# A four-layer convolution network on one core: weight preparation reordered, interval right products on two row tiles, Newton roots for the norms, image parts in eight transfers

## The chip, the cores and the metric

The kernel runs on one core of a Trainium2 chip. The time is the device time of one execution in microseconds (us). Three executions of the kernel before took 2478.43, 2479.14 and 2481.91 us; the median, 2479.14 us, is the number that the changed kernel is compared with.

A core has a matrix engine (PE), a vector engine (DVE), a scalar engine (ACT) and a general engine (POOL). Each works through its own list of instructions in order; where an instruction waits for a result of another engine, everything behind it on its own list waits too. SP, a fifth list, does no arithmetic: it issues nearly all DMA transfers of this kernel, also in order.

## The reference

The input x has 4 batches of 32x32 positions with 16 channels. Four layers each add to x a function of its group norm `_gn(x)` (8 groups of 2 channels; each group is divided by the square root of its variance plus 1e-5). Layers 0, 1 and 3 are convolutions in which every output position has its own 3x3x16x16 kernel G:

```python
first = jnp.einsum('ijyx,byxc->bijc', Msq, inputs)
...
diff = jax.nn.relu(inputs[:, None, None, :, :, :] - shifted)
second = L * jnp.einsum('ijyx,bijyxc->bijc', Wsq, diff)
return first - second
```

Here `shifted` is, for each of the 1024 output positions and each channel, a whole 32x32 image: the input convolved with the kernel of that position. Layer 3 (the last) does the same with another order of the axes of the input. Layer 2 is a dynamic program over intervals. Running maxima and minima over all intervals give a table r; two steps follow of the form `max over k of sigmoid(f[i,k] Wf + r[k,j] Wr + b)`, and then one last sigmoid of a product. The products with Wr are called right products below, those with Wf left products.

## The kernel before, in words

**Phases and steps.** The three convolution layers are done for two pairs of batches g (NG = 2): six phases, in the order (g, layer) = (0,0), (1,0), (0,1), (1,1), (0,2), (1,2). A phase has 8 chunks t of 128 output positions, and a chunk has 32 steps: 16 channels f times 2 images b. So there are 1536 steps. A step fills one PSUM tile of 128 positions x 1024 pixels (a pair of banks; four such tiles exist, tag "ps"). DVE then multiplies min(tile, 0) by the chunk's W and sums, in one instruction with its accumulator read (`second_part`, L680).

**A step on PE.** For accuracy, weights and images are split into an upper part and a remainder in the faster matmul type. `first_part` issues 8 matmuls with the image parts `ib` and `ia`; ACT then scales the PSUM tile in place (L663); `second_part` adds 6 matmuls with `iyz` and `im9`. All have 64 rows of contraction: they come in pairs, one on the upper and one on the lower half of the array's rows (a row tile each). `conv_layer` issues first_part of step k, then second_part of step k-1, so the scaling of one step hides behind the matmuls of its neighbours. The first 16 steps (units 0 and 1, "plain") use unsplit fp32 data and are longer.

**Units and slots.** The weights of 4 channels of one chunk are a unit u; a unit serves 8 steps. The generator `prep_parts` (L220) prepares the units two ahead. It is resumed once per step, so that a unit takes 8 steps, which are called slots 1 to 8 here. Slot 1: DVE cuts off the upper bits (L203). Slot 2: ACT L175. Slot 3: ACT L236, POOL L237 and L238. Slot 4: ACT L240, POOL L241 and four copies (L243, L245). Slot 5: POOL subtracts the identity from the raw weights of unit u+1 (`prep`, L214). Slot 7: SP moves a part to the other half of the partitions (L251, two transfers) and loads the raw weights of unit u+2 (`load_raw`, L110, 768 KB, into the buffer that unit u has just left).

**What runs behind.** All else runs as a second generator, `behind(phase)`, resumed at the end of a step. Its `yield n` waits n steps; `yield IDLE` waits for slot 1, 5, 6, 7 or 8, `yield CALM` for slot 6, 7 or 8. Behind a phase it makes the images of the next one: `group_norm` (L312), a turn of the result and its way through DRAM (L375 to L395), then per image b `split`, `place` and `difference`. Behind phases 3 and 4 it first does the interval layer (`interval_layer`, L484) for g = 0 and 1. The products with M come through `first_terms` (L418) behind phases 0, 2 and 5.

**The parts that the diff touches.** `place` (L290) copies quarters of the split image into `ia` and `ib` with 12 transfers per image. `group_norm` gets the variance sums on DVE (the last instruction is the transpose at L337), takes a square root on ACT (L358, after a one-element square root at L353 that pulls the function table in early), a reciprocal on DVE (L360) and multiplies on POOL (L361). The interval layer uses sigmoids on ACT, with a one-element one at L591 for the same reason. Its `right_side` (L555) makes three fp32 products of 352, 231 and 110 columns, one in each of three successive steps, each in its own PSUM tile and all on the upper row tile (L561), and ACT copies each into the table `rt` (L564). Steps of a chunk run through f, and within it through b; only the very first chunk is sorted so that 4 channels of image 0 come before those of image 1.

The norms whose sums end in slot 5 are those of the first two convolution layers (the waits between their parts are 4 steps). Those of the interval layer (waits of 2) and of the last convolution layer (waits of 1) end in slot 2.

Of the kernel before, what the change touches and what calls it, by code (L numbers as in the profile page):

```python
# [15 lines left out]
P = 128  # L16
# [3 lines left out]
GC = GB * C  # L20
# [24 lines left out]
def net_kernel(ctx: ExitStack, tc: tile.TileContext, x, xq, xi, convs, iv_w, iv_b, out):  # L45
# [174 lines left out]
    def prep_parts():  # L220
# [4 lines left out]
        for u in range(PLAIN, n_chunks * NU):  # L225
# [12 lines left out]
            nc.gpsimd.tensor_tensor(W9, W9.bitcast(F32), src[:, 2], ALU.add)  # L238
            yield ()
# [4 lines left out]
            for lo, hi in QUARTERS:  # L244
                nc.gpsimd.tensor_copy(WL[lo], high[hi])  # L245
            yield ()
            prep(u + 1)
# [7 lines left out]
            load_raw(u + RAWS)  # L255
# [14 lines left out]
    def halves(temp, b):  # L270
        v = temp.rearrange("p (k s b n) -> p k s b n", k=2, s=2, b=GB)
        return v[:, 0, :, b], v[:, 1, :, b]
# [36 lines left out]
    def pair_view(ap):  # L309
        return ap.rearrange("p t (g s) -> p t g s", s=2)  # L310

    def group_norm(g, name, dst, gap):  # L312
# [47 lines left out]
        nc.vector.reciprocal(rstd, rstd)  # L360
# [7 lines left out]
    def before_conv(g, layer):  # L368
# [29 lines left out]
        temp = big.tile([P, 8192], F32R, tag="big", name=f"temp_{g}{layer}")[:, :TEMP]  # L398
# [19 lines left out]
    def first_terms(layer, mt):  # L418
# [3 lines left out]
        for g in range(NG):  # L422
            for pt in range(NT):
                for j in range(4):
# [4 lines left out]
                    )  # L429
        ft = work.tile([P, NG, NT * GC], F32, tag="fs", name=f"ft_{layer}")  # L430
# [15 lines left out]
    def constants():  # L446
# [7 lines left out]
        nc.gpsimd.tensor_scalar_mul(mask2[GC : 2 * GC], mask2[GC : 2 * GC], -1.0)  # L454
# [23 lines left out]
        for k, name in ((1, "r0"), (4, "r1")):  # L478
            t = const.tile([64, NQ * GB, C], F32, name=name)
# [4 lines left out]
    def interval_layer(g):  # L484
# [56 lines left out]
        )  # L541
        yield 5
# [437 lines left out]
```

## Time and profile before

| what | us |
|---|---|
| three runs, median | 2479.14 |
| the profiled execution, its own time | 2478.41 |
| its span, first to last instruction | 2476.7 |
| PE matmul busy | 2458.2 |
| DVE busy | 2087.3 |
| ACT busy | 1878.4 |
| POOL busy | 1579.7 |
| L680, the mean of one of 1536 | 1.224, and 0.083 for the accumulator read |
| L663, the mean of one of 1520 | 1.008 |

"Busy" is the part of the span in which an engine worked. Matmuls are pipelined and their ends are modelled, so a PE that is busy at 99% may still run slower than it could: the starts of successive matmuls tell more. In an undisturbed stretch of the trace (starts from 537.66 to 935.74 us, 254 steps) a step takes 1.567 us. In the timeline a row gives start, duration, engine, line, operation, output <- inputs, and in brackets the idle time before it with what ended that.

### The profile page before, as it was taken

Reading aid. Unit: us, or ns where it says so; the run is one execution under the profiler, and the core shown is the slowest. Engines: PE = TensorE matmul, PEld = TensorE weight load, DVE = VectorE, ACT = ScalarE, POOL = GpSimd, SP = SyncE. Lnnn points to the kernel's source line nnn. Section 1 sums busy time; section 2 is a strip of 40 time slices with the busy share of each in tenths; the row PEclk is TensorE's granted clock in tenths of the full one; section 3 lists DMA queues with packets and bytes.
Section 4 is the critical chain, followed back from the end, with each engine's and each line's share of the span. In section 5 each row is a group of like instructions: output and inputs, shape, how many; then the busy total and the mean of one; then the engine's idle time right before and its main releaser. Section 6 shows DMA issues by size and latency. Waiting matters only on the chain.

```text
span 2476.7 us, 58058 instructions
## 1 busy us (share of the span) xinstructions
PE 2458.2 (99%) x21906; PEld 2090.1 (84%) x21906; DVE 2087.3 (84%) x3617; ACT 1878.4 (76%) x2181; POOL 1579.7 (64%) x1750
## 2 busy tenths in 40 slices
PE   8999999999999999999999999999999999999999
PEld 5999888888888888888888988888998888888887
DVE  9888878888888888778898988899889888788887
ACT  4778767787777778777777777787777787677776
POOL 4766655666565657555567777586878676555552
PEclk9999999999999999999999999999999999999999
DMA  6446754466454467644454545574455467554442
GB/s 198 138 137 182 203 155 135 124 182 164 133 143 135 135 168 198 186 116 134 136 145 127 142 124 140 146 196 125 126 138 144 127 181 195 154 148 137 137 137 54
DMA packets 97673, 366.92 MB, mean 148 GB/s; under 512 B 26480, under 2 KB 31472, under 8 KB 97392
## 3 DMA queue, kind: packets, MB, share of 16 engines
q1 hardware_dynamic: 96832, 362.79, 53.0%
q8 instruction: 172, 2.82, 0.5%
q14 instruction: 109, 0.89, 0.1%
q10 hardware_dynamic: 432, 0.39, 0.1%
q0 software_dynamic: 128, 0.02, 0.0%
HBM read 199.78 MB, written 1.02 MB: 81 GB/s over the span
## 4 chain that ended last, share of the span: by engine, by line
PE 94%; DVE 2%; issue 1%; DMA 1%; ACT 0%; SPq 0%; POOL 0%; ACTq 0%; DVEq 0%; POOLq 0%
PE pc L627 93%; DVE junk L680 1%; PE pf L425 1%; DMA raw<-in_g 1%; ACT pc L663 0%; DMA first<-in_g 0%; SPq L298 0%; DVE raw L846 0%; SPq L300 0%; PE ps_l L548 0%; PE ps_r L561 0%; DMA parts<-parts 0%; DVE tables L508 0%; DVE raw L854 0%; DMA ib<-first 0%
## 5 line engine op out<-in xcount | busy, mean ns | idle before, releaser
L680 DVE SCALAR_TENSOR_TENSOR junk<-pc,WT 128x1024 f32<-128x1024 f32 x1536 | 1879.5, 1224 | 359.1 <-PE pc L627 308.3
L663 ACT ACTIVATE pc<-pc 128x1024 f32<-128x1024 f32 x1520 | 1532.0, 1008 | 561.0 <-PE pc L627 535.8
L627 PE MATMUL pc<-ib,parts 64*128 64x512 f32 x6080 | 958.5, 388 | 4.1 <-DVE junk L680 3.4
L627 PE MATMUL pc<-iyz,parts 64*128 64x512 f32 x6080 | 955.5, 387 | 2.2 <-ACT pc L663 2.0
L627 PE MATMUL pc<-ia,parts 64*128 64x496 f32 x6080 | 933.5, 379 | 0.0
L627 PEld LDWEIGHTS pc<-ia,parts 64*128 64x128 f32 x6080 | 595.5, 184 | 100.8
L627 PEld LDWEIGHTS pc<-ib,parts 64*128 64x128 f32 x6080 | 591.5, 184 | 105.0 <-DVE junk L680 9.9
L627 PEld LDWEIGHTS pc<-iyz,parts 64*128 64x128 f32 x6080 | 592.5, 184 | 88.4 <-ACT pc L663 6.4
L627 PE MATMUL pc<-im,W 64*128 64x496 f32 x3072 | 611.5, 384 | 0.0
L237 POOL TENSOR_TENSOR parts<-raw,upper_w 128x512 fp32r<-128x512 f32 x190 | 248.5, 1308 | 500.2 <-DVE upper_w L203 434.8
L627 PEld LDWEIGHTS pc<-im,W 64*128 64x128 f32 x3072 | 303.0, 184 | 54.5 <-issue 3.2
L243 POOL CAST parts<-parts 32x512 fp32r<-32x512 f32 x380 | 231.1, 608 | 50.1 <-ACT parts L240 31.8
L238 POOL TENSOR_TENSOR W<-W,raw 128x512 fp32r<-128x512 f32 x190 | 247.6, 1303 | 1.8 <-ACT W L175 1.8
L241 POOL TENSOR_TENSOR parts<-parts 128x512 fp32r<-128x512 f32 x190 | 246.8, 1299 | 2.0 <-ACT parts L236 1.9
L245 POOL CAST parts<-upper_w 32x512 fp32r<-32x512 f32 x380 | 231.6, 609 | 22.8
L214 POOL TENSOR_TENSOR raw<-raw,ident 128x512 f32<-128x512 f32 x190 | 199.9, 1052 | 52.2 <-DMA raw<-in_g 28.7
L175 ACT ACTIVATE W<-raw,low_w 128x512 fp32r<-128x512 f32 x190 | 136.2, 717 | 0.1
L680 DVE DVE_READ_ACCUMULATOR junk<-pc,WT 128x1 f32 x1536 | 127.5, 83 | 0.0
L236 ACT ACTIVATE parts<-upper_w 128x512 fp32r<-128x512 f32 x190 | 118.8, 625 | 6.6 <-DVE upper_w L203 6.4
L240 ACT CAST parts<-upper_w 128x512 fp32r<-128x512 f32 x190 | 116.5, 613 | 0.0
L695 POOL TENSOR_SCALAR acc<-acc 128x32 f32<-128x32 f32 x40 | 16.4, 409 | 141.7 <-DVE junk L680 139.7
L203 DVE TENSOR_SCALAR upper_w<-raw 128x512 int32<-128x512 int32 x190 | 86.1, 453 | 1.2 <-POOL raw L214 0.9
(139 smaller groups left out, 479.4 us busy)
## 6 DMA issues: line engine op xcount, KB each, us to landing
raw<-in_g SPq DMA_DIRECT2D x190, 768.0 KB, 7.1
parts<-parts SPq DMA_DIRECT2D x380, 384.0 KB, 4.9
WT<-in_w SPq DMA_DIRECT2D x48, 512.0 KB, 4.6
MT<-in_mt SPq DMA_DIRECT2D x24, 512.0 KB, 7.4
raw<-xs SPq DMA_DIRECT2D x120, 71.8 KB, 2.9
ib<-temp SPq DMA_DIRECT2D x40, 128.0 KB, 2.6
ia<-temp SPq DMA_DIRECT2D x80, 62.0 KB, 3.4
ib<-first SPq DMA_DIRECT2D x8, 128.0 KB, 2.4
```

Source lines behind the costliest of these rows:

```text
L175: nc.scalar.activation(dst, src, AF.Copy, scale=mask[:, 1:2])
L214: eng.tensor_tensor(raws[u][:, s, at:to], raws[u][:, s, at:to], pick[s][:, f0 + at : f0 + to].unsqueeze(2).to_broadcast([P, to - at, P]), ...
L236: nc.scalar.activation(WD, high, AF.Copy, scale=-EPS)
L237: nc.gpsimd.tensor_tensor(WL, w8, high, ALU.subtract)
L238: nc.gpsimd.tensor_tensor(W9, W9.bitcast(F32), src[:, 2], ALU.add)
L240: nc.scalar.copy(WU, high)
L241: nc.gpsimd.tensor_tensor(WD, WD.bitcast(F32), WL.bitcast(F32), ALU.add)
L243: nc.gpsimd.tensor_copy(WU[hi], WL[lo].bitcast(F32))
L245: nc.gpsimd.tensor_copy(WL[lo], high[hi])
L627: nc.tensor.matmul(ps[:, h, at : at + n], lhsT=w[r], rhs=v[r] if n == NH else v[r][:, :n], start=first and k == 0, stop=k == len(pairs) - ...
L663: nc.scalar.activation(ps, ps, AF.Copy, scale=1.0 + EPS)
L680: nc.vector.scalar_tensor_tensor(junk, ps.rearrange("p h n -> p (h n)"), 0.0, chunks[n], op0=ALU.min, op1=ALU.mult, accum_out=accs[phase][ ...
```

## The change

- In `prep_parts`, `prep(u + 1)` moves from slot 5 to slot 3: on POOL it comes before L241 and the copies of unit u instead of after them. `load_raw(u + RAWS)` moves from slot 7 to slot 4: on SP it comes before the two transfers of the unit's parts, and before all that `behind` issues in slots 4 to 6.
- `place` does with 8 transfers what took 12, and those to `ib` come first.
- `inverse_root` takes the place of the root and the reciprocal: two integer-style instructions on DVE make a first guess, and four Newton rounds of four small instructions each follow on POOL. The waits between the rounds (1, 1, IDLE, 2 steps) add up to the old ones (2, IDLE, 2). The two one-element activations are gone, and one sigmoid of a single element stands in `first_terms` of layer 0.
- The right products: the weights `r0` and `r1` and the table r are also kept on partitions 64 to 127 (a POOL copy of 64 x 1089 per interval layer), and the three products are issued at once into the two banks of one PSUM tile, the first on the upper row tile, the other two on the lower. The three ACT copies stay in three successive steps.
- The first chunk of every phase is sorted like that of the first phase.

```diff
@@ prep_parts
             nc.gpsimd.tensor_tensor(W9, W9.bitcast(F32), src[:, 2], ALU.add)
+            prep(u + 1)
             yield ()
             nc.scalar.copy(WU, high)
             nc.gpsimd.tensor_tensor(WD, WD.bitcast(F32), WL.bitcast(F32), ALU.add)
...
                 nc.gpsimd.tensor_copy(WL[lo], high[hi])
+            load_raw(u + RAWS)
             yield ()
-            prep(u + 1)
             yield (IDLE,)
...
-            load_raw(u + RAWS)
             yield (IDLE, CALM)
@@ place
-        ty, tz = (v.bitcast(F32) for v in halves(temp, b))
+        parts = halves(temp.bitcast(F32)[:, :TEMP], b)
         da, db = (v[g].bitcast(F32)[:, :, b] for v in (ia, ib))
+        for lo, hi in QUARTERS:
+            for to, src in zip((lo, hi), parts):
+                nc.sync.dma_start(db[to], src[hi])
         for h, (lo, hi) in enumerate(QUARTERS):
-            for s in range(2):
-                at = HW if s == h else 0
-                for to, src in ((lo, ty), (hi, tz)):
-                    nc.sync.dma_start(da[to, s, :LAST], src[lo, s, at : at + LAST])
-            for to, src in ((lo, ty), (hi, tz)):
-                nc.sync.dma_start(db[to], src[hi])
+            for k, to in enumerate((lo, hi)):
+                at = (2 * k * GB + b) * NH + HW * (1 - h)
+                pitch = GB * NH + HW * (2 * h - 1)
+                src = temp.bitcast(F32)[lo, at : at + 2 * pitch].rearrange("p (s n) -> p s n", s=2)
+                nc.sync.dma_start(da[to, :, :LAST], src[:, :, :LAST])
@@ new function
+    def inverse_root(v, name):
+        n = GC // 2
...
+        nc.gpsimd.tensor_scalar(a, v, 1.0 / (2 * NP), 1e-5, op0=ALU.mult, op1=ALU.add)
+        nc.vector.tensor_scalar(
+            t.bitcast(I32), a.bitcast(I32), 1, None, op0=ALU.logical_shift_right
+        )
+        nc.vector.tensor_scalar(
+            y.bitcast(I32), t.bitcast(I32), -1.0, float(0x5F3759DF), op0=ALU.mult, op1=ALU.add
+        )
+        nc.gpsimd.tensor_scalar_mul(a, a, -0.5)
+        for pause in (1, 1, IDLE, 2):
+            yield pause
+            nc.gpsimd.tensor_tensor(t, a, y, ALU.mult)
+            nc.gpsimd.tensor_tensor(t, t, y, ALU.mult)
+            nc.gpsimd.tensor_scalar(t, t, 1.5, None, op0=ALU.add)
+            nc.gpsimd.tensor_tensor(y, y, t, ALU.mult)
+        return y
@@ group_norm
-        nc.scalar.activation(spare, spare, AF.Sqrt)
         v = yield from totals(f"v{name}")
-        yield 2
-        yield IDLE
-        rstd = work.tile([P, GC // 2], F32, tag="rstd", name=f"rstd_{name}")
-        nc.scalar.activation(rstd, v, AF.Sqrt, bias=eps, scale=1.0 / (2 * NP))
-        yield 2
-        nc.vector.reciprocal(rstd, rstd)
+        rstd = yield from inverse_root(v, name)
@@ first_terms, after the matmuls
+        if layer == 0:
+            nc.scalar.activation(spare, spare, AF.Sigmoid)
@@ interval_layer, after the table r is made
+        below = tables[R:, : T1 * T1].rearrange("p (i j) -> p i j", j=T1)
+        nc.gpsimd.tensor_copy(below, r[:R])
+        tops = (r[:R], below)
@@ right_side
-            for k0 in range(0, T1, 11):
+            ps = bank_pair(f"ps_{name}{g}")
+            blocks = []
+            for k0, h, at in ((0, 0, 0), (11, 1, 0), (22, 1, 11 * (T1 - 12))):
                 j0 = k0 + 1
-                ps = bank(f"ps_{name}{g}{k0}")
                 n = T1 - j0
+                blocks.append((k0, j0, n, ps[:, h, at : at + 11 * n]))
                 nc.tensor.matmul(
-                    ps[:, : 11 * n], lhsT=wr, rhs=r[:R, k0 : k0 + 11, j0:], start=True, stop=True
+                    blocks[-1][3], lhsT=wr[R * h : R * h + R], rhs=tops[h][:, k0 : k0 + 11, j0:],
+                    start=True, stop=True,
                 )
+            for k0, j0, n, sums in blocks:
                 nc.scalar.copy(
...
                 yield 1
@@ step of the interval layer
             yield IDLE
-            nc.scalar.activation(spare, spare, AF.Sigmoid)
             yield 2
@@ conv_layer
-            if n == 0:
+            if t == 0:
                 steps.sort(key=lambda s: (s[0] // FU, s[1]))
```

More of the change, by code (lines that the diff above doesn't have):

```diff
@@ L270, in halves @@
     def halves(temp, b):
-        v = temp.rearrange("p (k s b n) -> p k s b n", k=2, s=2, b=GB)
+        v = temp[:, :TEMP].rearrange("p (k s b n) -> p k s b n", k=2, s=2, b=GB)
         return v[:, 0, :, b], v[:, 1, :, b]
@@ L310, in pair_view @@
         return ap.rearrange("p t (g s) -> p t g s", s=2)
+    def inverse_root(v, name):
+        n = GC // 2
+        a, y, t = (
+            work.tile([P, n], F32, tag=tag, name=f"{tag}_{name}") for tag in ("root_a", "root_y", "root_t")
+        )
[5 more added lines that the diff above has]
+            y.bitcast(I32), t.bitcast(I32), -1.0, float(0x5F3759DF), op0=ALU.mult, op1=ALU.add
+        )
+        nc.gpsimd.tensor_scalar_mul(a, a, -0.5)
[6 more added lines that the diff above has]
+        return y
     def group_norm(g, name, dst, gap):
@@ L397, in before_conv @@
         yield 6 if layer == 2 else 12
-        temp = big.tile([P, 8192], F32R, tag="big", name=f"temp_{g}{layer}")[:, :TEMP]
+        temp = big.tile([P, 8192], F32R, tag="big", name=f"temp_{g}{layer}")
         for b in range(GB):
@@ L452, in constants @@
         )
-        nc.gpsimd.tensor_scalar_mul(mask2[GC : 2 * GC], mask2[GC : 2 * GC], -1.0)
+        for at in (GC, 3 * GC):
+            nc.gpsimd.tensor_scalar_mul(mask2[at : at + GC], mask2[at : at + GC], -1.0)
         yield 2
@@ L478, in constants @@
         for k, name in ((1, "r0"), (4, "r1")):
-            t = const.tile([64, NQ * GB, C], F32, name=name)
+            t = const.tile([P, NQ * GB, C], F32, name=name)
             for q in range(NQ):
@@ L555, in right_side @@
         def right_side(name, wr):
-            for k0 in range(0, T1, 11):
+            ps = bank_pair(f"ps_{name}{g}")
+            blocks = []
+            for k0, h, at in ((0, 0, 0), (11, 1, 0), (22, 1, 11 * (T1 - 12))):
                 j0 = k0 + 1
-                ps = bank(f"ps_{name}{g}{k0}")
                 n = T1 - j0
+                blocks.append((k0, j0, n, ps[:, h, at : at + 11 * n]))
                 nc.tensor.matmul(
-                    ps[:, : 11 * n], lhsT=wr, rhs=r[:R, k0 : k0 + 11, j0:], start=True, stop=True
+                    blocks[-1][3], lhsT=wr[R * h : R * h + R], rhs=tops[h][:, k0 : k0 + 11, j0:],
+                    start=True, stop=True,
                 )
+            for k0, j0, n, sums in blocks:
                 nc.scalar.copy(
-                    rt[:, j0:, k0 : k0 + 11],
-                    ps[:, : 11 * n].rearrange("p (k j) -> p j k", j=n),
+                    rt[:, j0:, k0 : k0 + 11], sums.rearrange("p (k j) -> p j k", j=n)
                 )
@@ L884, in rest_of_start @@
         yield 2
-        temp = first.bitcast(F32R)[:, used : used + TEMP]
+        temp = first.bitcast(F32R)[:, used:]
         for b in range(GB):
```

## The prediction

> **What bounds the kernel now.** I read the page's chain first, then PE's waits, then the chain in order of time, and the timeline around each break in it.
>
> ```profile
> PE 94%; DVE 2%; issue 1%; DMA 1%; ACT 0%; SPq 0%; POOL 0%; ACTq 0%; DVEq 0%; POOLq 0%
> PE pc L627 <- DVE junk L680: 3.4, 9, 0.5
> PE pc L627 <- ACT pc L663: 2.0, 5, 0.4
> ```
>
> PE carries the end. The waits look small, but matmul ends are modelled, so I measured starts: an undisturbed step takes 1.567 us, and 1520 split steps take 2382 of the 2476.7 us. The plain start (to 43.3 us) and three `first_terms` (7.04 us each) take 64, which leaves some 30 us: the interval layer's own products and about twenty short stops of PE. Nothing in the diff makes a step shorter, so only these 30 us can be had, and a new stop adds to them.
>
> The breaks that the change concerns:
>
> ```profile
> 1419.15 1.02 ACT pc L663
> 1422.63 13.54 PE pc L627 x118
> ...
> 1327.97 0.75 PE L561 MATMUL ps_r<-tables,r 64*128 64x352 f32 x2
> 1330.29 0.36 PE L561 MATMUL ps_r<-tables,r 64*128 64x231 f32 x1
> 1332.28 0.36 PE L561 MATMUL ps_r<-tables,r 64*128 64x110 f32 x2
> 1334.19 0.65 PE L548 MATMUL ps_l<-tables,f 64*32 64x264 f32 x8
> ...
> 1681.21 0.43 DVE L203 TENSOR_SCALAR upper_w<-raw 128x512 int32<-128x512 int32 x1
> 1681.78 1.30 POOL L237 TENSOR_TENSOR parts<-raw,upper_w 128x512 fp32r<-128x512 f32 x1 [5.46 <-DVE upper_w L203]
> 1684.07 0.21 DVE L337 STREAM_TRANSPOSE whole_vi<-total_vi 128x32 f32<-128x32 f32 x1
> 1691.46 0.68 POOL L361 TENSOR_TENSOR xi<-xc_i,rstd_i 128x256 f32<-128x256 f32 x1 [2.07 <-DVE rstd_i L360]
> 1695.83 1.31 DVE L508 STREAM_TRANSPOSE tables<-xi 32x256 f32<-32x256 f32 x2
> ```
>
> The first pair is a table load (1420.18, 1.283 us, L591) between two ACT rows: PE's next step starts 0.78 us late with the delay of its neighbours. The second group is one right side: three products, a step apart, then a left product. The third is an interval norm: POOL starts the unit's L237 at once, the variance sum is ready at 1684.28, and DVE wants the normed data at 1695.83.
>
> **What the Trainium skill says.** ScalarE: Activation LUTs, What ACT_TABLE_LOAD costs: about 1283 ns, and a drain with it, 2.66 us in all. The trace has 1283 ns; PE lost only 0.78, since ACT has slack. TensorEngine Tiling (Array Packing), Key Properties: different tiles execute in parallel. The trace agrees: at 1330.29 an L561 product on the upper rows and an `ib` matmul start together. GPSIMD Engine Reference, Specifications: POOL shares its SBUF interfaces with VectorE. It agrees: L203 takes 0.95 us at 1629.65 instead of 0.42 while L280 runs on POOL. Perfetto Trace Analysis, GPSIMD Engine Instruction, has POOL timed by the spacing of starts rather than by durations; L237's rows here last 1.30 and the next starts after 1.255, so below I use spacings. No page states what a small POOL instruction costs.
>
> **Right products.** From the first weight load of a right side to that of the left product, less three steps of 1.567, I find 1.73, 1.60, 1.75 and 1.60 us: 6.68 in all. After, the row tiles carry 352 and 341 columns at once. The 352 alone held PE 0.60 us (1327.97 to 1328.57), so about 0.65 each: **-4.0**. If they did not overlap, only the wait between them would go, about 0.45 each: -1.8. The one PSUM tile is held for three steps, which leaves three tiles to the steps. A step's L680 ends 1.31 us after its matmuls and a third tile is wanted 1.57 after them, so 0.1 to 0.2 is charged in the 0.65. The extra POOL copy costs 2.3 us (L534: 64x1024, 2.22). L538 ends at 1323.04, the product comes at 1327.97: hidden, by 2.6 us; the unit's parts behind it on POOL have several steps of room.
>
> **Table loads.** Four go (1420, 1564, 1832, 1976): 4 x 0.78 = **-3.1**. The new sigmoid's load stands behind 7.04 us of `first_terms` matmuls on PE, in which ACT has no tile to scale: 0; without that cover 0.78. The removed roots (0.30) and one-element calls (0.19) were not on the path.
>
> **Start.** PE waits for the last `ib` of image 1 at 50.52, 0.9 us late. SP is the cause: 12 issues an image at 0.6 us, stalled behind raw load 4 (L110 at 35.39). Now `ib` goes first, four issues fewer an image save 2.4 us of SP, and that load leaves in front of image 0, whose data have 7 us to spare. **-0.9**, bounds -0.9 to 0.
>
> **Subtraction and raw load.** POOL's sum per unit is unchanged (about 7.7 of 12.5 us). L241 and the copies, and so the parts' transfers, come 1.04 us later; they are wanted some nine steps after slot 7 and take 4.9 to land: hidden. On SP the load waits for L238 instead of standing behind the parts; what queues behind it are the parts (ready later anyway) and, in slots 4 to 6, transfers of `behind`. In phase 3 that ends a stop: the raw load at 1594.84 pushes in among the 24 image loads, DVE idles 1.65 us for `raw<-xs` (L203 at 1604.98), PE stops 0.8. Leaving before them, the load is out of the way: **-0.8**, bounds -1.2 to +0.8. The same place in phase 4 costs DVE 0.84 and PE nothing.
>
> **Sorting.** The last image transfers of phase 3 go out at 1638.78, the next phase begins at 1655.2; no phase border shows a stop. 0; were the images 16 us later, it would pay.
>
> **Newton.** This adds waits. POOL's first instruction waits for L337; queued behind it is the unit's POOL work. DVE's guess waits for that POOL instruction; queued behind it is L680, for which PSUM and PE wait. Of small POOL instructions the page has L344 (128x16, 0.253), followed 0.335 later by the one that needs it; for a two-input one I draw a line through L696 (128x32, 0.254) and L361 (128x256, 0.68): 0.22, with the same 0.08 of dependence 0.305. A round: 3 x 0.305 + 0.335 = 1.25.
>
> *Slot 5, four norms.* POOL ends its unit 0.3 us after L337, the guess comes some 1.0 us after it, and the rounds fall into idle POOL time before L361's slot. DVE is late by under 1.45 us, which PE bears: at 1605.94 L680 was 2.28 late and PE 0.81, so the slack is about 1.47. Cost 0.
>
> *Slot 2, interval, two norms.* From 1681.21 = 0: sum ready 3.07, guess and scaling done 3.93 (the unit used to begin at 0.57). Then L237, L238, L214 by start distances of 1.255, 1.251, 0.998: 7.43. Round one 8.68. L241 and four copies 1.38 + 2.69: 12.75. Three rounds: 16.5. L361: 17.2. DVE wants it at 14.62: it stands 2.6 us. The first L680 behind is 2.6 + 1.31 - 0.34 (its usual idling) = 3.57 late, PE 2.1; the second pair of transposes adds 1.31 - 0.26: 3.15, where 0.5 was lost. **+2.65 each.** The unit's parts leave at about 13 instead of 7, land at 19, and are wanted at 23: still hidden.
>
> *Slot 2, last layer's norms, two.* The sum is ready 3.5 after L203, behind more DVE work; without the table stop PE is ahead, and the guess makes DVE 1.87 late: 0.42. The normed data come 14.1 after the sum and L375 wants them 11.5 after: it stands 2.6, is 2.7 late in all, PE 1.25. **+1.67 each.**
>
> **Sum.** -4.0 - 3.1 - 0.9 - 0.8 + 5.3 + 3.3 = -0.2 on the span of 2476.7. The profiled execution took 2478.41 (1.7 outside the span), the median is 0.73 above it: 2479.14 - 0.2 = **2478.9**.
>
> **Rivals.** *Cheap rounds.* If POOL overlaps small instructions as in L459 (64x32, starts 0.198 apart), a round takes 0.8 and the data come 1.8 earlier: DVE stands 0.8, PE loses 0.85 and 0.42. Newton costs 2.5, the sum is -6.3: 2472.8. For it speaks L459; against it that each instruction needs the one before, as L346 needs L344.
>
> *Dear rounds: slower.* In the four slot-2 norms the rounds cost 0.42 an instruction instead of 0.31: 16 x 0.11 = 1.8 us more standing of DVE, all of it passed on to PE: +7.0, 2486. It passes +0.2% (4.96 us, about what measuring this kernel can tell from no change) from 0.39 per instruction on. For it: L695, 128x32, has a mean of 0.409 when DVE is busy; against it: L344, which is undisturbed in eight of eight.
>
> *The row tiles do not overlap.* The fp32 products take turns: +2.2 on the sum, 2481.1. Against it stands the start at 1330.29.
>
> **How the numbers follow.** Forecast 0.45, its own range 2475.5 to 2482.5 (a round of 1.15 to 1.34, start and raw load within bounds). Cheap rounds 0.25; dear rounds 0.18; no overlap 0.08; 0.04 for a wait in SP's or DVE's order that I missed, slower. Faster by over 0.2% is the cheap case and an edge of the forecast, 0.28; slower the dear case, the rest and edges, 0.25; within, 0.47. To hold 8 in 10 the range takes in the cheap case and half of the dear one: 2472 to 2485.5.
>
> **What would show it.** Right: L561 once per side, two row tiles starting within 0.3 us; table loads at two places only, the second under L425; no `ib` wait near 50; L508 after an idle DVE that waits for POOL L361 for 2 to 3 us, with a PE stop behind it; L375 the same in phases 3 and 4; POOL's L237 starting after L337 there. Wrong: L361 done before DVE asks (cheap), rounds over 1.5 us (dear), L237 not held by the new first instruction, or a new stop elsewhere, as of upper_x behind the raw load.

## The result and the profile after

The changed kernel takes 2488.89 us (median of six executions, 2486.37 to 2490.48), the kernel before 2479.53 in the same six rounds. The ratio is 1.0036, with a 95% interval of 1.0025 to 1.0047: 9.4 us slower, outside the predicted range of 2472.0 to 2485.5.

The span of the profiled execution grew from 2476.7 to 2487.6 us. In the changed file the matmuls of a step are L653 (before: L627), the min-and-sum is L706 (L680), ACT's scaling L689 (L663), the right products L587 (L561), the left ones L572 (L548), the norm's product L379 (L361), the turn of the interval data L529 (L508) and that of the image data L393 (L375).

The page of the changed kernel, part 4, the shares of the chain that ended last:

```profile
PE 92%; DVE 3%; POOL 2%; issue 1%; DMA 1%; SPq 1%; ACT 0%; ACTq 0%; DVEq 0%; POOLq 0%
```

PE had 94%. What it lost went to DVE, POOL and SP's queue. The waits of the changed kernel (engine and line, what it waited for, then us in total, times, longest):

```profile
POOL temp L280 <- DMA ia<-temp: 17.9, 5, 4.4
...
PE pc L653 <- DVE junk L706: 10.3, 15, 1.7
...
DVE xt L393 <- POOL xn L379: 5.0, 2, 2.5
DVE tables L529 <- POOL xi L379: 4.9, 2, 2.5
...
PE pc L653 <- DMA parts<-parts: 4.6, 4, 1.5
...
PE pc L653 <- ACT pc L689: 1.1, 2, 0.6
```

The two waits of DVE for the norms were predicted, with their size. The wait of PE for `parts` and that of L280 for `ia` were not; before has no wait of PE for `parts`. (A wait is named after what came last: three of the five at L280 contain 2.71 us in which POOL waits for DVE in the kernel before too.) The kernel before has these two in their place, the second at the start:

```profile
POOL temp L280 <- DVE upper_x L203: 8.1, 3, 2.7
...
PE pc L627 <- DMA ib<-first: 0.6, 1, 0.6
```

The norm of the interval layer in phase 4, from the timeline of the changed kernel:

```profile
1687.19 0.43 DVE L203 TENSOR_SCALAR upper_w<-raw 128x512 int32<-128x512 int32 x1
...
1690.03 0.21 DVE L361 STREAM_TRANSPOSE whole_vi<-total_vi 128x32 f32<-128x32 f32 x1
...
1690.41 0.20 POOL L320 TENSOR_SCALAR root_a_i<-whole_vi 128x16 f32<-128x16 f32 x1 [8.24 <-DVE whole_vi L361]
1690.64 0.17 DVE L321 TENSOR_SCALAR root_t_i<-root_a_i 128x16 int32<-128x16 int32 x1 [0.40 <-POOL root_a_i L320]
...
1691.12 1.29 POOL L237 TENSOR_TENSOR parts<-raw,upper_w 128x512 fp32r<-128x512 f32 x1
...
1694.62 0.21 POOL L330 TENSOR_TENSOR root_t_i<-root_a_i,root_y_i 128x16 f32<-128x16 f32 x1
...
1703.63 0.68 POOL L379 TENSOR_TENSOR xi<-xc_i,root_y_i 128x256 f32<-128x256 f32 x1
...
1704.34 1.26 DVE L529 STREAM_TRANSPOSE tables<-xi 32x256 f32<-32x256 f32 x2 [2.46 <-POOL xi L379]
```

L237 now starts 3.93 us after L203 (0.57 before), L379 ends 17.1 after it, and DVE stands for 2.46: the prediction had 3.93, 17.2 and 2.6. A right side of the changed kernel:

```profile
1331.99 0.77 PE L587 MATMUL ps_r<-tables,r 64*128 64x352 f32 x6
1332.56 0.73 PE L653 MATMUL pc<-ib,parts 64*128 64x512 f32 x4
...
1337.59 0.65 PE L572 MATMUL ps_l<-tables,f 64*32 64x264 f32 x8
```

The six records of the three products (two for each) start within 0.50 us, the first two of them together at 1331.99, and `ib` starts 0.57 us after them. Function tables are loaded in two places only, L858 at the start and L449, 1.283 us each.

To see where the time went I laid the starts of ACT's scaling in the two traces side by side, step by step, and took the median of each unit's eight differences. Between two units the difference stays put, or it jumps where a stop came or went:

| what | predicted, us | in the trace, us |
|---|---|---|
| start, to step 16 | -0.9 | +1.2 |
| second image, phases 1 and 2 | 0 | +0.8 |
| interval norms, two | +5.3 | +5.0 |
| last layer's norms: guess, and turn to `xt` | +3.3 | +0.5, +2.5 |
| table loads, four | -3.1 | -3.0 |
| right products, four sides | -4.0 | -2.2 |
| small stops at the interval scans | 0 | -0.8 |
| image loads and parts, phase 3 (units 124 to 127) | -0.8 | +3.2 |
| the same, phase 4 (units 156 to 159) | 0 | +3.6 |
| second image, phase 5 | 0 | +0.3 |
| sum | -0.2 | +11.0 |

The sum answers to the 10.9 us between the two spans; the medians differ by 9.4. The two rows of image loads and parts are the least certain: the trace of the right products alone (below), where nothing else was changed, also loses 2.5 us in phase 4 between steps 1248 and 1272. The unforeseen terms are in the chain of the changed kernel in order of time (start, us, what):

```profile
26.79 1.55 DVE first L280
...
33.15 2.38 DMA ia<-first
...
1601.69 5.15 DMA parts<-parts
1606.88 14.23 PE pc L653 x118
...
2024.64 9.44 DMA parts<-parts
...
2041.74 4.45 DMA ia<-temp
```

In phases 3 and 4 PE waits for parts that took 5.15 us (unit 124) and 9.44 us (unit 157) to land; in the kernel before, the same transfers took 5.29 and 5.07. At the start and in phase 4 an `ia` transfer of image 0 stands in the chain ahead of L280, which writes image 1.

### The profile page after: what moved, and what is told of

Its sections match the earlier page's. It is cut to its first block, busy times and chain, and to the rows that moved or that the text cites. A ratio compares the mean times of both kernels' runs of the same rounds, so it can differ in the third digit from the quotient of the medians.

```text
span 2487.6 us, 58093 instructions
## 1 busy us (share of the span) xinstructions
PE 2459.4 (99%) x21906; PEld 2047.3 (82%) x21906; DVE 2087.2 (84%) x3625; ACT 1871.5 (75%) x2159; POOL 1605.7 (65%) x1897
## 4 chain that ended last, share of the span: by engine, by line
PE 92%; DVE 3%; POOL 2%; issue 1%; DMA 1%; SPq 1%; ACT 0%; ACTq 0%; DVEq 0%; POOLq 0%
PE pc L653 90%; DVE junk L706 2%; PE pf L443 1%; DMA parts<-parts 1%; POOL parts L242 0%; ACT pc L689 0%; POOL parts L246 0%; POOL parts L244 0%; DMA first<-in_g 0%; POOL parts L237 0%; SPq L410 0%; POOL raw L214 0%; POOL W L238 0%; DMA ia<-temp 0%; SPq L296 0%
## 5 line engine op out<-in xcount | busy, mean ns | idle before, releaser
L706 DVE SCALAR_TENSOR_TENSOR junk<-pc,WT 128x1024 f32<-128x1024 f32 x1536 | 1879.3, 1223 | 354.8 <-PE pc L653 296.6
L689 ACT ACTIVATE pc<-pc 128x1024 f32<-128x1024 f32 x1520 | 1532.3, 1008 | 579.1 <-PE pc L653 553.2
L653 PE MATMUL pc<-ib,parts 64*128 64x512 f32 x6080 | 950.1, 388 | 15.4 <-DVE junk L706 10.3
L653 PE MATMUL pc<-iyz,parts 64*128 64x512 f32 x6080 | 944.8, 386 | 1.2 <-ACT pc L689 1.1
L653 PE MATMUL pc<-ia,parts 64*128 64x496 f32 x6080 | 923.8, 379 | 0.0
L653 PEld LDWEIGHTS pc<-ib,parts 64*128 64x128 f32 x6080 | 576.6, 184 | 131.7 <-DVE junk L706 19.7
L653 PEld LDWEIGHTS pc<-ia,parts 64*128 64x128 f32 x6080 | 579.8, 184 | 113.2
L653 PEld LDWEIGHTS pc<-iyz,parts 64*128 64x128 f32 x6080 | 577.7, 184 | 96.9 <-ACT pc L689 4.1
L653 PE MATMUL pc<-im,W 64*128 64x496 f32 x3072 | 601.5, 384 | 0.0
L237 POOL TENSOR_TENSOR parts<-raw,upper_w 128x512 fp32r<-128x512 f32 x190 | 246.3, 1296 | 513.6 <-PE pc L653 461.2
L653 PEld LDWEIGHTS pc<-im,W 64*128 64x128 f32 x3072 | 294.7, 184 | 60.5 <-issue 3.5
L238 POOL TENSOR_TENSOR W<-W,raw 128x512 fp32r<-128x512 f32 x190 | 248.1, 1306 | 1.1 <-ACT W L175 1.1
L214 POOL TENSOR_TENSOR raw<-raw,ident 128x512 f32<-128x512 f32 x190 | 200.6, 1056 | 3.6 <-DMA raw<-in_g 3.6
L706 DVE DVE_READ_ACCUMULATOR junk<-pc,WT 128x1 f32 x1536 | 127.2, 83 | 0.0
L241 ACT CAST parts<-upper_w 128x512 fp32r<-128x512 f32 x190 | 116.4, 613 | 0.0
L203 DVE TENSOR_SCALAR upper_w<-raw 128x512 int32<-128x512 int32 x190 | 83.7, 440 | 4.4 <-POOL parts L246 4.2
```

The source lines that it names most:

```text
L214: eng.tensor_tensor(raws[u][:, s, at:to], raws[u][:, s, at:to], pick[s][:, f0 + at : f0 + to].unsqueeze(2).to_broadcast([P, to - at, P]), ...
L237: nc.gpsimd.tensor_tensor(WL, w8, high, ALU.subtract)
L241: nc.scalar.copy(WU, high)
L653: nc.tensor.matmul(ps[:, h, at : at + n], lhsT=w[r], rhs=v[r] if n == NH else v[r][:, :n], start=first and k == 0, stop=k == len(pairs) - ...
L689: nc.scalar.activation(ps, ps, AF.Copy, scale=1.0 + EPS)
L706: nc.vector.scalar_tensor_tensor(junk, ps.rearrange("p h n -> p (h n)"), 0.0, chunks[n], op0=ALU.min, op1=ALU.mult, accum_out=accs[phase][ ...
```

## The experiments

Every median stands beside runs of the kernel before on the same chip, whose medians lay between 2478.1 and 2479.0 us. "+7.3" below is the difference of these two medians. Executions of one kernel lie up to 2 to 4 us from their median, and so do single profiles.

**Newton alone, and all but Newton.**

In the kernel before (and the other way round in the changed one):

```diff
-        nc.scalar.activation(spare, spare, AF.Sqrt)
         v = yield from totals(f"v{name}")
-        yield 2
-        yield IDLE
...
-        nc.scalar.activation(rstd, v, AF.Sqrt, bias=eps, scale=1.0 / (2 * NP))
-        yield 2
-        nc.vector.reciprocal(rstd, rstd)
+        rstd = yield from inverse_root(v, name)
```

> The kernel before with the Newton roots alone (and the sigmoid in the first products). Theory 'late norm': +5.0 (interval), +2.5 (xt), +0.5 (guess), -3.0 (table loads), -0.8 (scans) and the late parts of units 124 and 156 in full, about +4: some +8, 2487.5. Rival 'moved preparation': without the moved subtraction the parts are early enough; then +4.2, 2483.7. The prediction's own sum for this part, with nothing lost on SP: +5.5, 2485.

> The changed kernel with the square roots, the reciprocal and the one-element activations of before, all else as changed. Theory 'late norm': the Newton rounds make the interval norms and the last layer's norms late, and the late norm also pushes the image's transfers on SP ahead of the parts of units 124 and 156. Then 5.0 (interval), 2.5 (transpose to xt), 0.5 (guess) and about 4.7 (units 124 and 156 with what swings back after them) go, and 3.0 of table loads and 0.8 of smaller stops at the scans come back: 9 less, about 2480. Rival 'moved preparation': the units' late parts come from the subtraction that now stands ahead of the copies; then the stops at units 124 and 156 stay, and it is 4 to 5 less, about 2484.5.

Newton alone: 2485.99 us, +7.3, ratio 1.0027 (1.0016 to 1.0037). Old roots in the changed kernel: 2480.54, +1.9, ratio 1.0007 (0.9999 to 1.0015), so 7.5 less than the +9.4. Added or taken away, the Newton roots cost some 7.4 us, table loads already deducted. That is near "late norm", but the interval of the first (4.0 to 9.2 us) holds the other two expectations as well. The traces say more: PE waits 2.96 us for the parts of unit 124 in the changed kernel, 1.22 with Newton alone, and 0.38 with the old roots. But units 156 and 157 still wait 0.96 and 1.32: not all of that is Newton.

In the timeline of Newton alone the stall has another name, for the subtraction L214 is still in slot 5 there:

```profile
1280.79 1.04 POOL L214 TENSOR_TENSOR raw<-raw,ident 128x512 f32<-128x512 f32 x1
1281.87 0.43 DVE L203 TENSOR_SCALAR upper_w<-raw 128x512 int32<-128x512 int32 x1 [2.04 <-POOL raw L214]
...
1285.06 1.31 DVE L526 STREAM_TRANSPOSE tables<-xi 32x256 f32<-32x256 f32 x2 [0.26 <-POOL xi L377]
```

DVE stands 2.04 us for POOL's L214, which the rounds hold back, and then only 0.26 for the norm. PE loses 2.3 there, and 2.5 in the changed kernel: which of DVE's instructions meets the late POOL hardly matters.

**The right products alone** (that part of the change's diff in the kernel before).

> The kernel before with the right products of the change alone. By the traces of before and after, 0.55 us per right side: 2.2 less, about 2477.3. The prediction had 1.0 each: 4.0 less, 2475.5. If the trace's gain is partly lent by other parts of the change (PE that was late anyway), less than 1 us.

2476.16 us: -2.5, ratio 0.9992 (0.9984 to 1.0000). The trace has -0.52 to -0.58 a side, the changed kernel's -0.53 to -0.59: eight sides speak against the prediction's 1.0, which the interval of the medians alone would just admit. Starts of steps show why. Before, around the side at 1327.97, four steps and the left product took 8.36 us, which is 1.51 more than four steps of 1.567 and the 0.58 of the left product; after, 7.78, or 0.93 more. The second and third products of before cost little, 0.15 and 0.20 in the steps that they open, since they ran beside `ib` matmuls; and after, 0.3 us of small delays in the three following steps come on top of the 0.60. What these wait for the records don't show.

As a whole this trace, of the slowest of the 13 executions, gains nothing: it stands 2.0 us ahead of before at step 1240 and 0.5 behind at the end. 1.4 of that go at step 1269, where DVE's L203 takes 1.42 us beside POOL's L280 and PE waits for L687 (the min-and-sum there). So the stretch in which phase 4 loads its images can lose some 2 us without Newton roots, moves or a new `place`.

**The moved subtraction and raw load; the sorting** (each part of the diff in the kernel before).

> The kernel before with the subtraction in slot 3 and the raw load in slot 4, nothing else. Theory 'raw load ahead': in phase 4 the 768 KB load now goes out amid the image transfers and ahead of the parts of units 156 and 157, as with the old roots, where PE waited 0.96 and 1.32 us for parts; that run lost 3 us there. So +2 to +3, 2481.5, with waits of PE for parts in phase 4. The prediction had -0.8 here: 2478.

> The kernel before with the first chunk of every phase sorted, nothing else. Both theories: no change, within 1 us of the kernel before, as the prediction had it. A loss of more would be a part of the 9.4 us that is put down to others.

The moves alone: 2481.28 us, +2.4, ratio 1.0009 (1.0001 to 1.0017). Sorting alone: 2478.38, -0.5, ratio 0.9997 (0.9989 to 1.0005), no change. The predicted -0.8 for the moves is excluded by the interval. But the expected waits of PE for parts are not in this trace; its profiled execution took 2478.3, among this kernel's fastest, so where most of the 2.4 us arise is not shown. What all traces with the moves share is 0.5 us at the start (0.52 to 0.54 at step 16, counted from the first L203, in this kernel and in three others without the false wait below; -0.2 to +0.2 without the moves).

Next, only the load was put back in the changed kernel:

```diff
             for lo, hi in QUARTERS:
                 nc.gpsimd.tensor_copy(WL[lo], high[hi])
-            load_raw(u + RAWS)
             yield ()
...
+            load_raw(u + RAWS)
             yield (IDLE, CALM)
```

> The changed kernel with the raw load back in slot 7, behind the parts; the subtraction stays in slot 3. Theory 'raw load ahead': the start's remaining 0.4 us, the wait for the parts of unit 157 (0.9) and part of those of units 124 and 156 go: 2 to 3 less than the changed kernel, 2486.3. Rival: the load's place is worth the 0.8 us that the prediction counted, or nothing: 2489 to 2489.7.

2704.47 us, ratio 1.0910 (1.0895 to 1.0925). The waits of that kernel say why:

```profile
POOL raw L214 <- DMA raw<-in_g: 811.6, 172, 8.5
```

The subtraction in slot 3 needs a load that now leaves behind the parts of the unit before; these wait for copies that stand behind the previous subtraction. So the subtraction's move needs the load's (the reverse was not run), and neither expectation had looked at that ring.

**The eight transfers.** First the twelve old ones in the changed kernel, then the eight with another layout of the buffer:

```diff
-        v = temp[:, :TEMP].rearrange("p (k s b n) -> p k s b n", k=2, s=2, b=GB)
-        return v[:, 0, :, b], v[:, 1, :, b]
+        v = temp[:, :TEMP].rearrange("p (b k s n) -> p b k s n", b=GB, k=2, s=2)
+        return v[:, b, 0], v[:, b, 1]
...
-                at = (2 * k * GB + b) * NH + HW * (1 - h)
-                pitch = GB * NH + HW * (2 * h - 1)
+                at = 2 * (2 * b + k) * NH + HW * (1 - h)
+                pitch = NH + HW * (2 * h - 1)
```

> The changed kernel with the twelve image transfers of before. In the changed kernel's trace the image 1 instructions at L280 wait for `ia` transfers of image 0 (0.69 us on DVE at the start, 17.9 us in five waits on POOL), which none does in the kernel before. Theory 'false wait': the new `ia` source view runs across the other image's part of the buffer, so writing that part waits for the transfers. Then the losses at step 16 (1.17 us), at steps 344 and 600 (0.35 and 0.45), at 1272 and 1344 (1.52 and 0.31) go, and perhaps some of 1256 (0.92): 3.8 to 4.7 us less than the changed kernel, about 2484.6, and no wait of L280 for `ia`. Rival 'raw load': these delays come from the raw load that now goes out ahead of the image transfers; then the time stays within 1 us of 2488.9.

> The changed kernel with its eight transfers, but with the split image's buffer laid out image by image, so that an `ia` source view stays within its own image's half. Theory 'false wait': no L280 instruction waits for `ia` any more, and the time falls by as much as with the twelve old transfers or a little more: about 2 to 3.5 us less than the changed kernel, 2486. Rival 'order': the `ib`-first order or the larger transfers themselves cost the time; then it stays near 2488.9.

2486.06 us (+7.4, ratio 1.0028, 1.0017 to 1.0039) and 2485.52 (+6.7, ratio 1.0029, 1.0017 to 1.0041), where the changed kernel has 1.0036. By the medians, 2 to 3 us; the intervals overlap, but the traces agree. With the image-by-image layout no L280 waits for `ia` (the row reads 8.1, 3, 2.7 for DVE again, as before), and at step 16 there is +0.5 instead of +1.4 (from the first L203); the waits at L280 in phases 0 to 2 are 2.71 instead of 4.29, 4.00 and 4.41. So it is neither the order nor the number of transfers: a source view that strides over both images makes a write to image 1 wait until image 0 has been read.

**Newton on DVE.** In the changed kernel, with the scaling of the sum (`a`) and the guess on DVE at once, and three rounds:

```diff
-        nc.gpsimd.tensor_scalar_mul(a, a, -0.5)
-        for pause in (1, 1, IDLE, 2):
+        for pause in (1, IDLE, 2):
             yield pause
...
+            nc.vector.tensor_tensor(t, y, y, ALU.mult)
+            nc.vector.scalar_tensor_tensor(t, t, -0.5, a, op0=ALU.mult, op1=ALU.mult)
+            nc.vector.scalar_tensor_tensor(y, t, 1.5, y, op0=ALU.add, op1=ALU.mult)
```

> The changed kernel with the Newton rounds on DVE: three rounds of three instructions, none on POOL. Theory 'late norm': the norm is ready as early as before; 5.0 (interval), 2.5 (xt), 0.5 (guess) and some 3.5 at unit 124 go, the table loads stay saved, 0.8 comes back at the scans: about 2479 (the time with the old roots less 3, plus at most 1 for the extra DVE work). Rival 'DVE late': thirteen instructions of about 0.2 us a norm make DVE late past its slack of 1.47 us in the four norms of slot 2: +1 each, 2483.

2492.77 us, +13.9, ratio 1.0055 (1.0042 to 1.0067): worse than the change itself. Of the rounds most instructions took 0.17 to 0.22 us. The guess, in the first interval norm, did not:

```profile
1274.25 1.03 POOL L214 TENSOR_TENSOR raw<-raw,ident 128x512 f32<-128x512 f32 x1
1274.39 0.93 DVE L321 TENSOR_SCALAR root_t_i<-root_a_i 128x16 int32<-128x16 int32 x1
1275.25 1.28 POOL L242 TENSOR_TENSOR parts<-parts 128x512 fp32r<-128x512 f32 x1
1275.35 1.22 DVE L324 TENSOR_SCALAR root_y_i<-root_t_i 128x16 int32<-128x16 int32 x1
```

L321 and L324 last until the POOL instruction beside them ends; in the changed kernel, where POOL waits for the guess, the same instruction takes 0.17. With the first round behind it (0.27, 0.18 and 0.47) DVE was 3 us late, more than its slack of 1.47, and PE lost 2.0 to 2.3 in each of the four norms of slot 2. The Trainium skill offers a reason: by VectorE: DVE Perf Modes, What auto-detection actually checks, a DVE instruction with a single source in SBUF can take a mode that, by the walkthrough there, uses both read ports for one tensor, and the prediction quoted that POOL shares the interfaces. For the guess the trace agrees with that. Instructions with two inputs aren't spared either: those of 0.27 and 0.47 end with a POOL instruction too.

**Newton later.** All rounds in one go where the old root stood, in the changed kernel:

```diff
+        yield 2
+        yield IDLE
         nc.gpsimd.tensor_scalar(a, v, 1.0 / (2 * NP), 1e-5, op0=ALU.mult, op1=ALU.add)
...
-        for pause in (1, 1, IDLE, 2):
-            yield pause
+        for _ in range(4):
```

> The changed kernel with all of the Newton work (guess and four rounds on POOL, in one go) two steps and an IDLE later, where the old root stood; by then POOL is done with the unit. Theory 'late norm by place': what costs is that the first POOL instruction and the rounds are threaded through a unit's work, so that the unit waits for the sum and the rounds for the unit. Placed later, the data come 5.9 + 0.7 us after slot 5 begins, within 0.5 us of when DVE wants them: the stands (5.0 + 2.5), the guess (0.5) and the late transfers at unit 124 (about 3) go, the table loads stay saved. About 2479, as with the old roots less 3 plus some stops at the scans. Rival 'the rounds are too long anywhere': DVE stands as before and it stays at 2486 or more.

2490.21 us, +12.1, ratio 1.0048 (1.0035 to 1.0061). A miss, by both readings. In the interval layer it did what was expected, +0.8 each instead of +2.5. But in the norms of slot 5, which cost nothing in the changed kernel, the rounds now start just ahead of the next unit. From the timeline:

```profile
491.57 0.67 POOL L381 TENSOR_TENSOR xn<-xc_c,root_y_c 128x256 f32<-128x256 f32 x1
492.20 1.29 POOL L237 TENSOR_TENSOR parts<-raw,upper_w 128x512 fp32r<-128x512 f32 x1
...
509.32 0.49 PE L655 MATMUL pc<-ib,parts 64*128 64x512 f32 x1 [1.54 <-DMA parts<-parts]
```

L237 starts 6 us later than before (486.24), of which 2.5 are what this kernel was behind by then. The parts come too late, and PE stops 2.5 us at step 304, 1.4 at step 112 and 2.2 around step 560: a unit's preparation bears less delay than I had counted. And the stop at unit 124 did not go: step 992 lost 4.4 us.

Next, two parts in the kernel before: right products and these roots, with three rounds; then the same with `place` from the buffer laid out image by image; then, without that, each kind of norm in its own gap (slot 6 for the norms of slot 5, which `early` marks, the next slot 5 for those of slot 2, `a` and the guess on DVE):

```diff
-        yield 2
-        yield IDLE
-        nc.gpsimd.tensor_scalar(a, v, 1.0 / (2 * NP), 1e-5, op0=ALU.mult, op1=ALU.add)
+        if early:
+            yield 1
+        else:
+            yield 2
+            yield IDLE
+        nc.vector.tensor_scalar(a, v, 1.0 / (2 * NP), 1e-5, op0=ALU.mult, op1=ALU.add)
```

> The kernel before with two parts of the change alone: the right products, and the Newton roots in the later place, with three rounds. From right_alone -2.5, from the four table loads -3.0, stands nil: 2473.3. If the rounds cost as they do in the changed kernel: 2481.

> The kernel of right_and_newton_later with eight transfers in `place`, `ib` first, from the buffer laid out image by image. The prediction's -0.9 at the start supposed that SP is the cause of the wait for `ib` at 50.52; without false waits and without the moved raw load it should now come: 2472.4. If the start only turns to another wait: 2473.3.

> The kernel before with the right products, and with Newton roots placed where POOL is idle: the guess on DVE, three rounds of four POOL instructions in one go, in slot 6 for the norms of slot 5 and in slot 5 of the next turn for those of slot 2. Theory 'place, not length': no stop over 1 us in the norms of slot 5 (run newton_later lost up to 2.5 each there), and less than 0.5 each in those of slot 2; so -2.5 and -3.0 with about 1 lost: 2474.5. Rival 'length': any 16 dependent instructions on POOL push its units late: 2479 or more.

2479.00 us (+0.9, ratio 1.0002, 0.9994 to 1.0010), 2479.85 (+1.7, 1.0007, 0.9999 to 1.0015) and 2477.69 (-1.2, 0.9993, 0.9985 to 1.0001). So the mended `place` gains nothing, and "place, not length" holds for the most part: the last one's norms of slot 2 still lose 0.8 to 0.9 in the interval layer, and those of slot 5 show no stop of their own. It stood 5.2 us ahead of before at step 1224, and 2.8 at the end: the gain shrinks where phase 4 loads its images, as that of the right products alone did.

> The whole change with the Newton roots placed as in newton_where_idle and the split image's buffer laid out image by image. If the parts add up (right products -2.5, table loads -3.0, moved subtraction and raw load +2.4, stops +1): 2476.6. If the moved subtraction and raw load hurt more with the image transfers of phases 3 and 4: 2480.

The whole change with both mends: 2480.50 us, +1.6, ratio 1.0009 (1.0000 to 1.0017), the dearer of the two expectations. Step 992 alone loses 3.3 us, though against PE's steps its norm is only 0.9 us late.

**The stop at units 124 and 156.** For each profile I took how late `xt` is turned and how late the second transfer of the unit's parts leaves, both against the kernel before and less what PE as a whole was ahead or behind at steps 976 and 1232; and how long SP took to issue the first twelve image loads (`raw<-xs`). Of the names, newton_where_idle is the last of the three kernels above, same_and_place_apart the second, change_mended the whole change with both mends, and roots_as_before the changed kernel with the old roots. All in us, for phase 3; phase 4:

| kernel | `xt` late by | twelve loads take | parts leave late by | PE waits for parts, total |
|---|---|---|---|---|
| before | 0; 0 | 5.3; 6.3 | 0; 0 | 0 |
| moves_alone | 0; 0.4 | 6.3; 7.5 | 0.5; 1.8 | 0 |
| newton_alone | 2.6; 2.6 | 5.4; 6.1 | 2.5; 2.5 | 1.2 |
| newton_where_idle | 0.3; 1.4 | 5.3; 6.6 | -0.4; 1.6 | 0 |
| same_and_place_apart | 1.7; 1.2 | 5.3; 6.8 | 2.5; 1.7 | 2.1 |
| roots_as_before | 0; 0.4 | 6.7; 8.5 | 1.0; 2.8 | 2.6 |
| change_mended | 0.9; 0.9 | 7.4; 7.4 | 3.4; 2.2 | 2.0 |
| changed | 2.7; 2.7 | 7.0; 7.4 | 6.0; 4.1 | 4.6 |

Two things add up. With the moves a raw load of 768 KB stands ahead of these twelve on SP, and they take 1 to 2 us longer. With the Newton roots as changed `xt` comes 2.6 to 2.7 late. The parts leave behind both. Moves alone let PE wait for no parts, the roots alone 1.2 us, all but the roots 2.6, and the whole change 4.6. Before, the second transfer of unit 124 left 6.1 us before PE used it (the median over all units is 14.2) and landed after 5.3: 0.8 us to spare. How long the parts take to land varies too: unit 124's took between 5.1 and 7.4 us where SP issues them, 7.1 in same_and_place_apart, where PE waited 2.1. I have no explanation for that.

For units 125 and 157 the runs show one. With the moved load SP issues a raw load directly ahead of their parts, and the second transfer lands 7.2 to 10.4 us after its issue in all eleven kernels that have the moved load; in the nine without it, it lands after 5.0 to 5.2.

Three kernels try to take the parts out of that place, the first so:

```diff
-                nc.sync.dma_start(
+                eng = nc.scalar if u in (124, 156) else nc.sync
+                eng.dma_start(
```

The second has `nc.gpsimd` for `nc.scalar`; in the third, and in the last run, the two transfers of every unit are issued in slot 5 instead of slot 7.

> The changed kernel with the two transfers of the parts of units 124 and 156 alone on ACT's queue instead of SP's. Theory 'SP's order': these parts wait on SP behind the image transfers that the late norm lets out; off SP they leave some 5 us earlier, PE does not wait at steps 992 and 1248, and 3 to 4.5 us go: 2485. Rival 'the transfers themselves': the bytes of the image transfers and the raw load slow them wherever they are issued: 2488 or more.

2493.85 us, +15.7, ratio 1.0061 (1.0049 to 1.0074); it tells nothing of SP, as the trace of that kernel shows:

```profile
1592.60 1.15 ACTq L253 DMA_DIRECT2D parts<-parts  x2
...
1593.85 1.01 ACT L690 ACTIVATE pc<-pc 128x1024 f32<-128x1024 f32 x1 [4.78 <-issue]
```

ACT itself stood 4.8 us, until POOL's last copy, and PE behind it. A transfer that waits on an engine's list stops that engine.

> The changed kernel with the two transfers of the parts of units 124 and 156 alone on POOL's queue, right behind these units' own copies, instead of SP's. Theory 'SP's order': they leave some 5 us earlier, PE does not wait for parts at steps 992 and 1248, and 3 to 4.5 us go against the changed kernel: 2485. Rival 'the transfers themselves': the image transfers and the raw load slow them wherever they are issued, and PE waits for these parts as before: 2488 or more.

2487.70 us, +8.8, ratio 1.0033 (1.0020 to 1.0045). The second transfer of unit 124's parts left at 1594.05, 7.6 us earlier than in the changed kernel, and PE did not wait at step 992, where the changed kernel lost 3.1: that stop was SP's order. The rival is right in part: among the image loads the transfer took 9.4 us to land, so only 3.4 of the 7.6 us were won. And one unit later:

```profile
1617.01 0.50 PE L654 MATMUL pc<-ib,parts 64*128 64x512 f32 x1 [0.64 <-DMA parts<-parts]
...
1618.66 0.49 PE L654 MATMUL pc<-ib,parts 64*128 64x512 f32 x1 [1.16 <-DMA parts<-parts]
```

Unit 125's parts left from 1609.4 on, behind the other twelve image loads and another raw load, and steps 1000 to 1016 lost 3.8 us.

> The changed kernel with each unit's two part transfers issued in slot 5 instead of slot 7. Theory 'SP's order': in phases 3 and 4 they stand ahead of eight of the twelve image transfers; the copies of unit 124 end at 1593, so they leave at 1593 instead of 1600, and the stops at units 124, 156 and 157 (3.1, 1.5 and 0.9 us) go for the most part: 2485. Rival 'too much in any order': the image transfers come later by as much and the stop moves to the images or to unit 125, as with the parts on POOL's queue: 2488.

> The kernel of newton_where_idle with the part transfers in slot 5. Its trace loses 2.1 us in phase 4 from step 1248 to 1272, where the gain of 4.9 us up to there meets the transfers. 'SP's order': up to 2 us of it come back, 2475.7. 'Too much in any order', or SP now standing in front of the image transfers until the copies are done: 2477.7 or more.

2505.17 us (ratio 1.0106, 1.0092 to 1.0119) and 2482.96 (1.0010, 1.0002 to 1.0019). Against the changed kernel, step 992 won 3.0 and step 1248 won 1.5; steps 1000 and 1256 lost 2.2 and 2.9, and phases 0 to 2 lost 7, 5 and 5 us in the stretches that load images. There POOL's L237 waits 16.1 us in all for `raw<-xs`; that SP holds up the image loads behind the parts, while it waits for a unit's copies, is likely, but not shown. "Too much in any order" fits: between the norm and the next chunk SP and the transfers have 8 + 24 image transfers, two or three raw loads and two pairs of parts to bring through. A late start of that queue is paid at one unit or the next.

No kernel here is faster than the one before by more than the measurement can tell. The best medians are those of right_alone and newton_where_idle.

## Why the prediction was wrong

**The Newton rounds: right in mechanism and size, wrong in where it ended.** A round takes 1.25 us, its instructions start 0.30 to 0.34 apart, and interval norms (+5.0 against +5.3), `xt` with the guess (+3.0 against +3.3) and the table loads (-3.0 against -3.1) came as worked out. Cheap and dear rounds are both refuted. The norms of slot 5 cost nothing, as said. In sum this part was to cost 5.5 and costs 7.3 to 7.5 by the medians, with an interval of 4.0 to 9.2 for the first. The step that failed is the end of the account for the last layer, "it stands 2.6, is 2.7 late in all, PE 1.25". The standing came true (2.5, `xt` 2.7 late, and +1.2 on PE), but I followed the late data into DVE and stopped there, and the sum has nothing for what the late `xt` holds up on SP. Behind L393 on SP stand 8 transfers to DRAM and the 24 image loads, and behind the first twelve of those the unit's parts; for those of unit 124 PE waits 2.96 us in the changed kernel and 0.38 with the old roots. What the stall makes late next had a second answer, on SP. (The prediction quoted 2.66 us for a switch of tables with its drain. In the kernel before, ACT ended a scaling at 1420.16 and began the next call at 1421.47, so the load took 1.31 us of ACT in all.)

**"On SP the load waits for L238 instead of standing behind the parts; what queues behind it are the parts (ready later anyway)", -0.8, bounds -1.2 to +0.8: false.** Measured for both moves +2.4, with an interval of 0.2 to 4.2. DVE's wait of 1.65 us for `raw<-xs` did go, but the load now goes out ahead of the image loads and of the parts that matter more there. The step that failed is "they are wanted some nine steps after slot 7 and take 4.9 to land: hidden". It holds for the median unit (14.2 us). But seven units that are prepared while images load (18, 42, 74, 124, 125, 156, 157) had 6.1 to 7.3 us from the leaving of their second transfer to its use, and the moves let the parts of units 124 and 156 leave 0.5 and 1.8 us later and those of units 125 and 157 land 3 us later and more. How this sums up to +2.4 is not shown: PE's trace with the moves alone has only the 0.5 at the start.

**"SP is the cause. -0.9, bounds -0.9 to 0": false, outside its bounds.** The wait for `ib` at 50.52 is gone as predicted. One step later PE loses 0.9 again, with DVE behind it in the chain (L706, then ACT's L689): DVE was the next bound. (With the mended `place` in the kernel before, the start gains nothing either: +0.2.) On top come the moves, 0.5, and the false wait, 0.8. I had read the new `ia` view for its number of transfers, not for the memory that it spans.

**Right products: -4.0, measured -2.2 in the trace and -2.5 alone.** The products overlap, so that rival is refuted. Two terms were mis-sized: the cost before, 1.51 at the side looked at where I had 1.67 on average, and the 0.65 after, which is 0.93. The POOL copy took 1.09 us, not 2.3, and is hidden.

**Sorting:** 0, as measured.

By parts, from medians: Newton +7.3, moves +2.4, right products -2.5, sorting -0.5, `place` +2.0 (9.4 less 7.4) make +8.7 of +9.4. Against the prediction's own parts the deviations are +1.8, +3.2, +1.5, -0.5 and +2.9 (the start's -0.9 set against `place`): no single surprise, but four terms that all went the same way. Each of these medians is uncertain by some 2 to 3 us, so which of them is largest is not settled. The case that came nearest is the one that had 0.04, a wait in SP's order that I missed; the false wait stood in no case. That the dear rounds' 2486 lies near the result is chance: their 0.42 us an instruction was 0.30 to 0.34.

## What to carry to other kernels

When data come late, follow them through every list that they feed, to the transfers that stand behind them, before a delay is called hidden; a margin read from the median unit (14.2 us here) says nothing of the seven that have 6 to 7. A transfer moved forward in a queue is paid by what it passes, in the time to leave and in the time to land. And a strided view counts, for the waits that it creates, as all that it spans: lay the buffer out so that a view stays within its own part.

## What was unexpected of the hardware

- A one-source DVE instruction of 128x16 took 0.17 us with POOL idle, and 0.93 and 1.22 beside POOL's 128x512 instructions, to the end of these. Those of the rounds beside POOL's 32x512 copies took 0.18 to 0.47.
- The second of a unit's two transfers of 384 KB landed 5.0 to 5.2 us after its issue for units 125 and 157 in nine kernels, and 7.2 to 10.4 us in the eleven where a raw load of 768 KB was issued directly ahead of the two.
- A source view that strides over both images made a write to the other image wait, 1.3 to 1.7 us more in three waits of POOL; laid out image by image, the waits went.
- The first loads of an execution differ: the first L203 started between 21.0 and 23.2 us in these traces, as much as many of the effects studied.
